# Adjacency transposed by DMA in 16-bit halves, filters loaded in nine 2 KB slots: one graph layer on one Trainium2 core

## The chip, the core and the metric

The kernel runs on one core of a Trainium2 chip. The core has a matrix engine (TensorE, PE in the profile, with its weight loads shown apart as PEld), a vector engine (VectorE, DVE), a scalar engine (ScalarE, ACT), GpSimd (POOL) and a sync engine (SP). SP, ACT and POOL also issue DMAs, each to a queue of its own (q1 is SP's, q10 ACT's, q0 POOL's in the profile); 16 DMA engines serve them all. Each engine runs its own list of instructions in order and waits on semaphores for the others.

The metric is the device time of one execution in microseconds (us). Lower is better. Seven runs of the kernel before took 1943.19 to 1951.11 us, median 1947.83.

## The reference

64 graphs of 256 nodes with 256 features (`x`, 64 x 256 x 256) and one symmetric 0/1 matrix per graph (`adj`, float32). Cut to what is computed:

```python
h = max(layernorm(x), 0)
# x_conv: 1-tap convolution over the nodes, batch norm, relu, 17-tap convolution, batch norm, + h, relu
s    = h @ w_se.T + b_se                                   # 3 numbers per node
dist = sq[:, :, None] + sq[:, None, :] - 2 * einsum('bnd,bmd->bnm', s, s)
A    = exp(-dist) * adj
msg  = relu(h @ w_msg.T + b_msg)
x_nmp = einsum('bnm,bmd->bnd', A, msg)
# gated recurrent unit over [x_conv, x_nmp] and h; result added to x
r, z = sigmoid(gi_r + gh_r), sigmoid(gi_z + gh_z)
out  = x + (1 - z) * tanh(gi_n + r * gh_n) + z * h
```

Everything is float32. `dist` is symmetric in its two node indices.

## The kernel before

Graphs are handled in pairs (`G = 2`, 512 columns), eight graphs (four pairs, `PB = 4`) make a batch, and there are eight batches (`NB`). The loop at lines 843 to 938 runs over the batches; in its body `i` is the batch's first pair and `nxt = i + 4` the first of the next batch, whose preparation is mixed in. The order of instructions is written out by hand (`manual_schedule`); the vector steps of a fast Fourier transform are put between other work by a small planner (`Pace`) that adds up estimated times of PE and DVE.

**Startup** (lines 390 to 841). The 17-tap filters are brought to the frequency domain with matmuls (`filters`), copied by ACT into `fo` (six buffers) and written to DRAM as `filt`, through SP's queue and in part POOL's. The filters do not fit on chip and are read back in each batch.

**A batch, product phase.** 16 frequency bins, two for each call of `products(b, m)`, m from 0 to 7. A bin has three kinds of filter (two in bin 15), 2 KB per partition and kind: 47 kinds in a batch. `load_bin` (line 591) loads a bin with one DMA on SP's queue into one of three buffers of 6 KB (`wb`); each bin is asked for three bins ahead of its use. `products` multiplies each kind by its operand (`Sv`, `V`, `U`, `PT`, results of the forward transform, which DVE computes), ACT copies one accumulator (`p`), DVE combines them into `Yv` and `Yu`. Between the calls stand parts of the graph work:

- `message(i)` (line 659): `msg` and the small embeddings `Z`; `embed(i)` (line 682) transposes `Z` into `ZT`.
- `affinity(i)` (line 689): four matmuls from `ZT`, ACT takes the exponential into `E`, DVE multiplies by `ADJ` (line 703), and then POOL's queue gets the two loads of the next pair's `adj` (`load_adj`, line 382; 2 KB rows).
- `transpose_a(i)` (line 707): A is needed with its second node index on partitions. Eight 128 x 128 transposes on PE (line 713) and two copies by ACT (line 714) make `AT`.
- `aggregate(i)` (line 716): `msg` times `AT`, eight matmuls (16 in the profile, since a float32 matmul shows as two), and two ACT copies into `XNM` (line 724).
- `finish(i)` (line 774): transposes the result of a pair back, DVE adds `x`, POOL's queue writes it out and loads `y` for a later pair.

`affinity(i)` stands after `products(b, 1)`, `transpose_a(i)` after `products(b, 2)`, `aggregate(i)` after `products(b, 3)`; the second pair follows in the same way after products 5, 6 and 7.

**A batch, gate phase.** `gates(i, dc)` (line 730) for four pairs and two halves: 18 matmuls of 512 columns each, ACT's `gn`, `tr`, `nn`, `tz`, DVE's `d`. Between them stand the graph work of pairs `i + 2` and `i + 3`, and for the next batch `transpose_h` (line 533; it also issues the load of `x` two pairs on, on SP's queue), `conv1` and the first steps of the Fourier transform.

Rows of a graph lie on partitions in the order `(h c)` after a view `(b h c)` (line 359): partition `16 h + b`, two rows `c` each. The tile `T` is scratch for the Fourier transform and first written by DVE when the forward transform begins.

Of the kernel before, what the change touches and what calls it, by code (L numbers as in the profile page):

```python
# [12 lines left out]

FP = mybir.dt.float32
AF = mybir.ActivationFunctionType
ALU = mybir.AluOpType
# [284 lines left out]
def kernel(  # L301
# [26 lines left out]
    nc = tc.nc  # L328
    P = 128
    B, N, D = x.shape  # L330
# [50 lines left out]

    def load_adj(i, eng=nc.gpsimd):
        ADJ[i] = work.tile([P, G * MC, N], FP, name="adj")
        load_rows(ADJ[i], adj, i, eng)

# [30 lines left out]

    HT, MSG, E, AT, XNM = {}, {}, {}, {}, {}

# [171 lines left out]

    def load_bin(b, n):
        b, n = b + n // BINS, n % BINS
        if b < NB:
            WB[b, n] = work.tile([P, 3, DC, D], FP, name="wb", bufs=3)
            kinds, m = 3 if n < BINS - 1 else 2, n // len(PASSES[0])
            first = 3 * (n - PASSES[m][0])
            nc.sync.dma_start(out=WB[b, n][:, :kinds], in_=filt[m][:, first:first + kinds])

# [13 lines left out]

    def products(b, m):
        load_bin(b, 2 * m + 2)
        p = [acc() for _ in range(3)]
        for n in range(2):
            for kind, v in enumerate(operands(2 * m + n)):
                if v is None:
                    continue
                for o in range(DC):  # L620
                    for k in range(DC):
                        mm(p[kind][:, (n * DC + o) * P:(n * DC + o + 1) * P],
                           WB[b, 2 * m + n][:, kind, k, o * P:(o + 1) * P],
                           v[:, k::DC, 0, :], P, start=(k == 0), stop=(k == DC - 1))
        load_bin(b, 2 * m + 3)
        p1 = work.tile([P, W], FP, name="p1")
        pv = [t.rearrange("p (n a e) -> p a n e", n=2, e=NW) for t in (p1, p[1], p[2])]
        if m < 7:
            nc.scalar.copy(p1, p[0])  # L629
            if m < 4:  # L630
                re, im = Yv(m % 2, m // 2 * 2, 2), Yv(m % 2, 4 + m // 2 * 2, 2)
            elif m < 6:
                re, im = Yu(m - 4, 0, 2), Yu(m - 4, 2, 2)
            else:
                t = Yu.t[:, :, :, 6:8, :].rearrange("p a c n e -> p n a c e")
                re, im = t[:, 0], t[:, 1]
            pace.vector(2 * W, pace.pe + PSUM)
            nc.vector.tensor_sub(re, pv[0], pv[2])
            nc.vector.tensor_add(im, pv[0], pv[1])
        else:  # L640
            half = W // 2
            nc.scalar.copy(p1[:, :half], p[0][:, :half])
            nc.scalar.mul(Yu(0, 4)[:, :, 0, :], p[0][:, half:].rearrange("p (a e) -> p a e", e=NW), 0.5)
            nc.scalar.mul(Yu(1, 4)[:, :, 0, :], p[1][:, half:].rearrange("p (a e) -> p a e", e=NW), 0.5)
            pace.vector(W, pace.pe + PSUM)
            nc.vector.tensor_sub(Yu(0, 5)[:, :, 0], pv[0][:, :, 0], pv[2][:, :, 0])
            nc.vector.tensor_add(Yu(1, 5)[:, :, 0], pv[0][:, :, 0], pv[1][:, :, 0])
# [41 lines left out]
    def affinity(i, early=False):  # L689
# [9 lines left out]
        for g in range(G):  # L699
            for c in range(MC):  # L700
                pace.vector(N, pace.pe + ACT)
                e = E[i][:, g, c].rearrange("p (c h b) -> p c h b", c=MC, b=NW)
                nc.vector.tensor_mul(e, e, ADJ[i][:, g * MC + c].rearrange("p (b h c) -> p c h b", c=MC, b=NW))
        if i + 1 < B // G:
            load_adj(i + 1)

    def transpose_a(i):
        AT[i] = late.tile([P, G, MC, N], FP, name="aT")
        for g in range(G):
            q = aux()  # L710
            for c in range(MC):
                for r in range(MC):
                    transpose(q[:, c * N + r * P:c * N + (r + 1) * P], E[i][:, g, r, c * P:(c + 1) * P])
            nc.scalar.copy(AT[i][:, g].rearrange("p c n -> p (c n)"), q)

    def aggregate(i):
        XNM[i] = late.tile([P, DC, W], FP, name="xnm", bufs=2)
        for dc in range(DC):
            p = aux()
            for g in range(G):  # L720
                for c in range(MC):
                    mm(graph(p, g), MSG[i][:, g, c, dc * P:(dc + 1) * P], AT[i][:, g, c, :], N,
                       start=(c == 0), stop=(c == MC - 1))
            nc.scalar.activation(XNM[i][:, dc, :], p, AF.Copy)


# [3 lines left out]
    def gates(i, dc, wait=None, early=None):  # L730
# [10 lines left out]
        product(ghn, h, n, True, True)  # L741
        gn = late.tile([P, W], FP, name="gn", bufs=2)
        nc.scalar.activation(gn, ghn, AF.Identity, bias=b_hh[:, 2 * DC + dc:2 * DC + dc + 1])
# [15 lines left out]
        nc.vector.scalar_tensor_tensor(gn, gn, 0.5, pn, op0=ALU.mult, op1=ALU.add)  # L759
        nn = late.tile([P, W], FP, name="nn", bufs=2)  # L760
        nc.scalar.activation(nn, gn, AF.Tanh, bias=b_ih[:, 2 * DC + dc:2 * DC + dc + 1])
# [51 lines left out]
    for t, v in ((b_msg[:, :D], msg_b), (b_msg[:, D:], se_b)):  # L813
        nc.gpsimd.dma_start(out=t, in_=bass.AP(tensor=v.tensor, offset=v.offset, ap=[[0, P], [1, v.shape[0]]]))
    load_adj(0, nc.sync)
    bn2 = bn_vecs(bn2, "bn2")
    b_ih, b_hh = vec(ih_b, "b_ih"), vec(hh_b, "b_hh")
    for j in range(PB):
        if j > 0:
            transpose_h(j)  # L820
        if 0 < j < PB - 1:
            norm(j + 1)
        conv1(j)
        run(split_steps(j))
        for m, n in steps[j * 4:(j + 1) * 4]:
            filters(m, n, nc.sync)
    s2, h2_shift = fold_bn(bn2, "bn2", 1.0 / L)
    b_rz = const.tile([P, 2 * DC], FP)
# [4 lines left out]
    for j, (m, n) in enumerate(steps[PB * 4:]):  # L833
        filters(m, n, nc.gpsimd if j % 2 else nc.sync)
        if j + PB * 4 == 2 * NG - 10:
            load_bin(0, 0)
            load_bin(0, 1)
    stage_ctx.close()
    late = ctx.enter_context(tc.tile_pool(name="late", bufs=1, reuse_waits="tile"))
    Yvt = late.tile([P, SL], FP, name="Yv")  # L840
    Yv = Slots(Yvt, GB * DC, L // 2, NW)
    pace.flush(odd)
    for b in range(NB):
        i = b * PB
# [4 lines left out]
        embed(i)  # L849
        if b > 0:  # L850
            finish(i - 1)
        products(b, 1)
        pace.add(fft.branch_back(Yv, T, 0))
        affinity(i)
        products(b, 2)
        transpose_a(i)
        products(b, 3)
# [12 lines left out]
        norm(nxt)  # L870
        affinity(i + 1)
        products(b, 6)
        transpose_a(i + 1)
        products(b, 7)
# [12 lines left out]
        join(3)  # L887
        aggregate(i + 1)
        transpose_h(nxt)
        message(i + 2)  # L890
# [3 lines left out]
        def wait(j=0):  # L894
            pace.flush(joined[j])
        gates(i, 0, wait, lambda i=i: affinity(i + 2, True))
        if b == 0:
            load_y(0)
            load_y(1)
        transpose_a(i + 2)  # L900
        gates(i, 1)
        pace.flush(normed)
        transpose_h(nxt + 1)
# [7 lines left out]
        pace.flush(joined[1])  # L911
        gates(i + 1, 0)
        pace.flush(normed)
        transpose_h(nxt + 2)
# [7 lines left out]
        embed(i + 3)  # L922
        gates(i + 1, 1)
        affinity(i + 3)
        gates(i + 2, 0)
        pace.flush(normed)
        transpose_h(nxt + 3)
        transpose_a(i + 3)
        conv1(nxt + 3)
# [55 lines left out]
```

## Time and profile before

The profiled execution took 1943.19 us, of which its span, from the first instruction to the last, is 1941.4.

| what | us |
|---|---|
| median of seven runs | 1947.83 |
| the profiled execution | 1943.19 |
| its span | 1941.4 |
| PE idle in the first 110 us | 32.1 |
| 256 transposes of `e` on PE, busy (line 712 to 713) | 38.3 |
| 64 copies `aT` on ACT (line 714), 0.59 each | 35.0 |
| 128 products `e * adj` on DVE (line 703) | 67.6 |
| PE and its weight loads waiting for `wb`, in all | 25.1 |
| SP issues of `wb` (128, 120 of them 768 KB) | 0.32 each |
| POOL issues of `adj` (62, 256 KB) | 0.60 each, 5.9 to landing |

The busy times of one engine overlap where it works as a pipeline, so a busy time is not always what an instruction adds to the list; the distance between two starts is. The granted clock of PE was 0.993 on average. A wait is named by the event that came last before the instruction began.

### The profile page before, as it was taken

To read this page: it belongs to the slowest core of one execution; us is meant where nothing else is said; L and a number is where in the kernel's file an instruction comes from. 1 tells how busy PE (TensorE), PEld (TensorE's weight loads), DVE (VectorE), ACT (ScalarE), POOL (GpSimd) and SP (SyncE) were. 2 spreads that over 40 slices of the span, in tenths; PEclk is the share of its full clock that TensorE was granted. 3 is DMA by queue.
4 is the path that set the end of the run, shared out by engine and by line. 5 is a ranking of instruction groups with operands and counts; after the bars stand their busy time and mean duration, and the time that the engine had idled before them with its cause. 6 is when DMAs were issued, how large, how long until landed. Compare 5 with 4: busy or idle time off the path is not lost.

```text
span 1941.4 us, 21503 instructions
## 1 busy us (share of the span) xinstructions
PE 1864.3 (96%) x7940; PEld 1161.3 (60%) x7940; DVE 1398.0 (72%) x2667; ACT 602.8 (31%) x1338; POOL 173.4 (9%) x266
## 2 busy tenths in 40 slices
PE   4999999999999999999999999999999999999997
PEld 2687544865468545774548654595546844577543
DVE  2888649985598946997489865898469884699522
ACT  1534331243222522243222432224322342224321
POOL 2110010000100010100000001000000000010000
PEclk9999999999999999999999999999999999999999
DMA  5784131721227112550126402172123711153010
GB/s 172 242 264 141 34 78 35 221 83 33 71 62 242 32 34 60 142 173 22 44 60 195 121 22 71 32 231 74 44 60 84 221 46 29 27 156 127 0 44 22
DMA packets 67938, 187.14 MB, mean 96 GB/s; under 512 B 20466, under 2 KB 25330, under 8 KB 67833
## 3 DMA queue, kind: packets, MB, share of 16 engines
q1 hardware_dynamic: 33884, 125.60, 19.5%
q0 software_dynamic: 29504, 56.50, 12.7%
q10 hardware_dynamic: 4445, 3.67, 0.6%
q8 instruction: 62, 1.02, 0.2%
q14 instruction: 43, 0.35, 0.1%
HBM read 156.54 MB, written 29.10 MB: 96 GB/s over the span
## 4 chain that ended last, share of the span: by engine, by line
PE 71%; DVE 15%; DMA 6%; ACT 4%; issue 3%; POOL 0%; DVEq 0%; ACTq 0%; POOLq 0%
PE acc L408 60%; PE aux L408 6%; DMA wb<-filt 4%; PE aux L412 3%; DVE T L64 2%; DMA taps<-in_c_wT_dram 1%; ACT Yv L656 1%; PE aux L696 1%; DVE Yv L61 1%; DVE Yv L58 1%; DVE U L64 1%; DVE PT L61 1%; DVE T L61 1%; DVE Sv L61 1%; DVE msg L668 1%
## 5 line engine op out<-in xcount | busy, mean ns | idle before, releaser
L408 PE MATMUL acc<-hT,w_hh 128*128 128x512 f32 x768 | 355.2, 597 | 0.0
L408 PE MATMUL acc<-xnm,w_ih 128*128 128x512 f32 x768 | 352.2, 595 | 0.0
L408 PE MATMUL acc<-Yv,w_ih 128*128 128x512 f32 x768 | 340.0, 592 | 0.0
L408 PEld LDWEIGHTS acc<-xnm,w_ih 128*128 128x128 f32 x768 | 146.9, 191 | 185.9 <-issue 185.9
L408 PEld LDWEIGHTS acc<-Yv,w_ih 128*128 128x128 f32 x768 | 145.9, 190 | 183.7 <-issue 183.0
L408 PEld LDWEIGHTS acc<-hT,w_hh 128*128 128x128 f32 x768 | 141.8, 190 | 158.4 <-issue 153.8
L756 DVE SCALAR_TENSOR_TENSOR gn<-tr,gn 128x512 f32<-128x512 f32 x64 | 44.2, 691 | 243.2 <-ACT tr L754 243.2
L754 ACT ACTIVATE tr<-acc,b_rz 128x512 f32<-128x512 f32 x64 | 44.0, 687 | 563.1 <-PE acc L408 563.1
L408 PE MATMUL acc<-hT,w_c 128*128 128x512 f32 x256 | 118.4, 606 | 14.5 <-ACT hT L541 14.5
L408 PE MATMUL acc<-U,wb 128*128 128x128 f32 x1024 | 123.5, 276 | 3.0 <-DMA wb<-filt 2.5
L408 PE MATMUL aux<-w_msg,hT 128*128 128x259 f32 x512 | 121.6, 385 | 4.2 <-DVE msg L668 4.2
L408 PE MATMUL acc<-V,wb 128*128 128x128 f32 x1024 | 124.8, 275 | 0.0
L408 PEld LDWEIGHTS acc<-U,wb 128*128 128x128 f32 x1024 | 119.1, 192 | 7.9 <-issue 2.7
L58 DVE SCALAR_TENSOR_TENSOR V<-T,V 128x256 f32<-128x256 f32 (+2 forms) x224 | 120.4, 607 | 0.3
L408 PEld LDWEIGHTS acc<-V,wb 128*128 128x128 f32 x1024 | 119.5, 192 | 0.0
L408 PE MATMUL aux<-aT,msg 128*128 128x256 f32 x512 | 117.4, 380 | 0.8
L408 PEld LDWEIGHTS aux<-w_msg,hT 128*128 128x128 f32 x512 | 94.1, 189 | 26.8 <-DVE msg L668 9.7
L782 POOL DMA_DIRECT2D out_dram<-y x64 | 39.0, 614 | 763.5 <-DVE y L781 762.2
L408 PEld LDWEIGHTS aux<-aT,msg 128*128 128x128 f32 x512 | 95.0, 190 | 18.8 <-issue 4.1
L408 PEld LDWEIGHTS acc<-hT,w_c 128*128 128x128 f32 x256 | 48.9, 195 | 64.4 <-issue 43.7
L64 DVE TENSOR_TENSOR V<-h 128x512 f32<-128x512 f32 x64 | 43.8, 684 | 54.7 <-ACT h L554 54.7
L629 ACT COPY p<-acc 128x512 f32<-128x512 f32 x56 | 32.8, 585 | 149.2 <-PE acc L408 74.4
(134 smaller groups left out, 2610.9 us busy)
## 6 DMA issues: line engine op xcount, KB each, us to landing
wb<-filt SPq DMA_DIRECT2D x120, 768.0 KB
y<-in_x_dram POOLq DMA_DIRECT2D x64, 256.0 KB, 5.7
out_dram<-y POOLq DMA_DIRECT2D x64, 256.0 KB, 4.7
adj<-in_adj_dram POOLq DMA_DIRECT2D x62, 256.0 KB, 5.9
x<-in_x_dram SPq DMA_DIRECT2D x60, 256.0 KB
filt<-fo SPq DMA_DIRECT2D x26, 252.0 KB
wb<-filt SPq DMA_DIRECT2D x8, 512.0 KB
filt<-fo POOLq DMA_DIRECT2D x10, 252.0 KB, 5.0
```

The source lines that it names most:

```text
L58: return self.step(out, lambda: self.v.scalar_tensor_tensor(out, x, s, y, op0=ALU.mult, op1=ALU.add))
L61: return self.step(out, lambda: self.v.tensor_add(out, x, y))
L64: return self.step(out, lambda: self.v.tensor_sub(out, x, y))
L408: nc.tensor.matmul(p, w, v, **kw)
L412: nc.tensor.transpose(p, v, ident)
L629: nc.scalar.copy(p1, p[0])
L656: nc.scalar.activation(v, v, AF.Relu, bias=h2_shift[:, o:o + 1])
L668: nc.vector.tensor_add(MSG[i][:, g, c, :], p[:, :D + SE], b_msg)
L696: nc.tensor.matmul(p[:, :N], ZT[rows_q, :P], ZT[rows_q, P:], start=True, stop=True)
L754: nc.scalar.activation(tr, pr, AF.Tanh, bias=b_rz[:, dc:dc + 1], scale=0.5)
L756: nc.vector.scalar_tensor_tensor(gn, tr, 1.0, gn, op0=ALU.add, op1=ALU.mult)
L782: nc.gpsimd.dma_start(out=rows(out, G * i + g), in_=row_tile(Y[i], g))
```

## The change

1. `transpose_a` and `AT` are gone. `aggregate` multiplies by `E` itself. As `dist` is symmetric, A^T is the exponential times the transposed `adj`; `ADJ` now holds `adj` transposed.
2. The transposed `adj` is made by DMA. Seen as 16-bit numbers a graph's `adj` is 256 x 512. `turn_adj` transposes it from DRAM to SBUF with one DMA transpose per graph on SP's queue (`HALVES`: column halves on partitions). `keep_adj` writes it to a DRAM buffer in eight DMAs of 128 pieces of 512 B, `load_adj` reads it back in eight DMAs of 128 pieces of 512 B with the rows on the right partitions (`ADJH`), all on SP's queue, and `join_adj` puts the two 16-bit halves together into `ADJ` with two ACT copies. The first two pairs use `T` as the place for `HALVES`.
3. The filters come one kind at a time: 376 DMAs of 256 KB into nine slots of 2 KB per partition, each asked for as soon as the kind nine places before it has been used. Before the first batch three bins are loaded instead of two.
4. Order: `finish(i - 1)` moves from after `products(b, 0)` to after `products(b, 2)`; `transpose_h(nxt)` from after `aggregate(i + 1)` to after `products(b, 6)`; the turns, writes and loads of `adj` are put into the batch by hand, the two loads of the product phase after `affinity(i)` and `affinity(i + 1)`. `gn` and `nn` have one buffer instead of two.

```diff
+    def turn_adj(i):
+        if i >= B // G:
+            return
+        if i < 2:
+            HALVES[i] = Tt.bitcast(U16).rearrange("p (i g k n) -> p i g k n", i=2, g=G, n=N)[:, i]
+        else:
+            HALVES[i] = late.tile([P, G, 2 * MC, N], U16, name="halves")
+        for g in range(G):
+            nc.sync.dma_start_transpose(out=HALVES[i][:, g], in_=adj[G * i + g].bitcast(U16))
+
+    def keep_adj(i):
...
+        ADJD[i] = dram.tile([G, L // 2, MC, 2, NW, N], U16, name="halves_d", bufs=6)
+        v = ADJD[i].rearrange("g h c j (k a) n -> g k a (h c j) n", a=4)
+        for g in range(G):
+            for k in range(2 * MC):
+                nc.sync.dma_start(out=v[g, k], in_=HALVES[i][:, g, k])
+
+    def load_adj(i):
...
+        ADJH[i] = late.tile([P, G, MC, 2, N], U16, name="adjh")
+        v = ADJD[i].rearrange("g h c j b n -> g c j h b n")
+        for g in range(G):
+            for c in range(MC):
+                for j in range(2):
+                    nc.sync.dma_start(out=ADJH[i][:, g, c, j], in_=v[g, c, j])
+
+    def join_adj(i):
...
         ADJ[i] = work.tile([P, G * MC, N], FP, name="adj")
-        load_rows(ADJ[i], adj, i, eng)
+        v = ADJ[i].bitcast(U16).rearrange("p q (n j) -> p j q n", j=2)
+        for j in range(2):
+            nc.scalar.copy(v[:, j], ADJH[i][:, :, :, j].rearrange("p g c n -> p (g c) n"))
...
-    def load_bin(b, n):
+    def load_kind(b, n, kind):
         b, n = b + n // BINS, n % BINS
-        if b < NB:
-            WB[b, n] = work.tile([P, 3, DC, D], FP, name="wb", bufs=3)
-            kinds, m = 3 if n < BINS - 1 else 2, n // len(PASSES[0])
-            first = 3 * (n - PASSES[m][0])
-            nc.sync.dma_start(out=WB[b, n][:, :kinds], in_=filt[m][:, first:first + kinds])
+        if b < NB and (n < BINS - 1 or kind < 2):
+            WB[b, n, kind] = work.tile([P, DC, D], FP, name="wb", bufs=9)
+            m = n // len(PASSES[0])
+            nc.sync.dma_start(out=WB[b, n, kind], in_=filt[m][:, 3 * (n - PASSES[m][0]) + kind])
...
     def products(b, m):
-        load_bin(b, 2 * m + 2)
...
-        load_bin(b, 2 * m + 3)
+                load_kind(b, 2 * m + n + 3, kind)
...
-        if i + 1 < B // G:
-            load_adj(i + 1)
...
-                    mm(graph(p, g), MSG[i][:, g, c, dc * P:(dc + 1) * P], AT[i][:, g, c, :], N,
+                    mm(graph(p, g), MSG[i][:, g, c, dc * P:(dc + 1) * P], E[i][:, g, c, :], N,
                        start=(c == 0), stop=(c == MC - 1))
             nc.scalar.activation(XNM[i][:, dc, :], p, AF.Copy)
+        if join:
+            join_adj(i + 1)
...
-    load_adj(0, nc.sync)
+    turn_adj(0)
+    turn_adj(1)
...
             filters(m, n, nc.sync)
+        if j < 2:
+            keep_adj(j)
...
     pace.flush(odd)
+    load_adj(0)
+    join_adj(0)
     for b in range(NB):
...
         affinity(i)
+        load_adj(i + 1)
         products(b, 2)
-        transpose_a(i)
+        if b > 0:
+            finish(i - 1)
         products(b, 3)
...
         affinity(i + 1)
+        if b > 0:
+            load_adj(i + 2)
+        else:
+            turn_adj(2)
         products(b, 6)
-        transpose_a(i + 1)
+        if b == 0:
+            keep_adj(2)
+            turn_adj(3)
+        transpose_h(nxt)
         products(b, 7)
...
+        load_adj(i + 3)
+        turn_adj(nxt)
...
         gates(i, 1)
+        keep_adj(nxt)
+        turn_adj(nxt + 1)
...
         gates(i + 1, 0)
+        keep_adj(nxt + 1)
+        turn_adj(nxt + 2)
...
         gates(i + 1, 1)
+        keep_adj(nxt + 2)
+        turn_adj(nxt + 3)
         affinity(i + 3)
+        load_adj(nxt)
         gates(i + 2, 0)
+        keep_adj(nxt + 3)
```

In the first batch `load_adj(2)` and `keep_adj(3)` come after the joins are queued, ahead of `aggregate(i + 1)`, and `join_adj(2)` comes in the `early` call of `gates(i, 0)`; in the other batches `join_adj(i + 1)` is the end of each `aggregate(i)`.

## The prediction

> **What bounds the kernel now.** I read the page first, busy time and the chain that ended last:
>
> ```profile
> span 1941.4 us, 21503 instructions
> PE 1864.3 (96%) x7940; PEld 1161.3 (60%) x7940; DVE 1398.0 (72%) x2667; ACT 602.8 (31%) x1338; POOL 173.4 (9%) x266
> ...
> PE 71%; DVE 15%; DMA 6%; ACT 4%; issue 3%; POOL 0%; DVEq 0%; ACTq 0%; POOLq 0%
> ```
>
> TensorE (PE) sets the pace; what shortens its instruction list shortens the end, unless PE then waits. By the timeline a batch lasts 229.2 us and repeats. The stage windows of the batch that starts at 570.23 us (columns: stretch, its length, busy time of PE, weight load, DVE, ACT, POOL, granted clock, DMA share, GB/s) split it into a product phase, to the second `aggregate`, and a gate phase:
>
> ```profile
> 570.23:627.70 57.47, 54.98 (x455) 52.04 (x454) 52.46 (x113) 15.85 (x49) 5.91 (x9) 1.00 0.72 225
> 627.70:799.44 171.74, 170.01 (x512) 87.70 (x511) 121.87 (x220) 55.34 (x112) 13.08 (x19) 1.00 0.18 46
> ```
>
> The reader sees two different stages. In the gate phase PE is 99% busy and DMA 18%: transfers there are free. In the product phase PE, DVE (52.46 of 57.47) and DMA are all near their limits, and it is where the filters stream through SP's queue. Two waits on PE matter, seen in PE's timeline: the one for a filter, and in the gate phase the price of eight transposes of `e`, which is the distance between the two starts, 0.87 us:
>
> ```profile
> 587.25 1.16 PE L408 MATMUL acc<-Sv,wb 128*128 128x128 f32 x8 [1.42 <-DMA wb<-filt]
> ...
> 428.43 1.04 PE L412 MATMUL aux<-ident,e 128*128 128x128 f32 x8
> 429.30 1.88 PE L408 MATMUL acc<-hT,w_hh 128*128 128x512 f32 x4
> ```
>
> Last I asked what one hardware queue delivers. The DMA views of five short stretches give its packets, MB and share of the 16 engines; in this order: `x` rows of 2 KB (405.5 to 407.5 us), `fo` rows of 2 KB (66 to 70), `wb` rows of 6 KB (586 to 589), `taps` rows of 1 KB on SP (8 to 12), single 4-byte elements on ACT's queue (3 to 6):
>
> ```profile
> q1 hardware_dynamic: 197, 0.38, 50.3%
> ...
> q1 hardware_dynamic: 427, 0.80, 64.4%
> ...
> q1 hardware_dynamic: 209, 1.16, 99.2%
> ...
> q1 hardware_dynamic: 440, 0.60, 40.7%
> ...
> q10 hardware_dynamic: 544, 0.00, 9.7%
> ```
>
> That is 99, 107, 70, 110 and 181 packets a us. With 6 KB packets the engines are full (99%, 387 GB/s); with 1 and 2 KB the queue stops near 100 to 110 packets a us while the engines are only 41 to 64% busy. So on this queue a small packet costs about 10 ns whatever it holds, and 2 KB packets give 190 to 200 GB/s.
>
> **The change, part by part.** *Transposes and their copy removed.* Per batch four `transpose_a`, two in each phase: 2 x 0.87 = 1.74 us off PE in the gate phase and as much in the product phase. 64 copies `aT` of 0.59 us leave ACT.
>
> *Filters in nine 2 KB slots.* The bytes are the same, but each bin's 128 packets of 6 KB become 3 x 128 of 2 KB. PE eats a kind in 0.89 us (a bin from 570.23 to 572.91 is 2.68 us), the queue brings one in 128/100 = 1.28 us. Of 47 kinds nine are there when the phase begins, so 38 x 128 = 4864 packets must pass: 48.6 us. Alone this fits: PE needs 57.47 less the transposes 1.74, the filter wait 1.42 and the small wait on `e` 0.2, so 54.1 us.
>
> *`load_adj` on SP, in that stream.* It left POOL's queue (two issues of 0.60 us, which nothing waits for) and is now eight DMAs of 128 pieces of 512 B. Both of a batch's product-phase calls, after `affinity(i)` and `affinity(i+1)`, stand in SP's order before filters: behind the first wait kinds 21 to 26, behind the second kinds 45 and 46. No 512 B row is in the trace; bounds are 97 packets a us (the 2 KB row's slow end) and 181 (the 4-byte row); I take 130, as it is nearer to the 1 KB row. 2048 / 130 = 15.8 us. The phase cannot end before the queue: first slot free 0.9, from a freed slot to data 1.7 (572.9 to the first packets about 574.5), 48.6 + 15.8, landing about 0.5, last kind 0.9: 68.4 us against 57.5, **+10.9 us**. Bounds: 110 and 181 give 59.5 (+2.0), 97 for both gives 75.2 (+17.7); a queue that is no limit gives 54.1 (-3.4). In stalls: PE waits about 6 to 9 us ahead of kind 21, in `products(b, 3)`, and 3 to 9 ahead of kind 45, in `products(b, 7)`.
>
> [...]
>
> *Turning and storing adj.* Per pair two DMA transposes, eight `keep_adj` writes and a wait between them, all on SP, in the gate phase from the second batch's data on. 1024 pieces at 130 a us are 7.9 us per `keep_adj`. No transpose by DMA is in the trace; of 256 KB the bounds are 0.7 us (387 GB/s) and 9.3 us (1024 pieces of 256 B at 110 a us). I take 2 us, nearer the low end, since the bytes are those of an `x` load, whose 256 packets take 2.6. Queue work in the gate phase: 8 x 2 + 4 x 7.9 + 2 x 7.9 + eight `x` loads of 2.6 = 84 of 171.7 us, hidden behind PE's gates. Behind a waiting `keep_adj` stand the next turn and an `x` load, which is needed some 30 us after its issue (445.82, statistics at 478.02). Were the cover gone, SP would be late with `load_adj(nxt)`, and ACT would stand in `join_adj`.
>
> [...]
>
> *`join_adj` on ACT.* Two copies of 1024 columns; the row `aT` has 0.59 us for 512 and `e` 0.38 for 256, so about 1.0 us each. ACT is 31% busy. Behind it stands `p` (603.53 while `xnm` ended at 600.5, room for 2 us). Only at the head of the gates is ACT tight (PE waited 0.74 us for `zT`): bounds 0 and 0.9 us a batch, I take 0.5.
>
> *Nothing:* `finish` between products 2 and 3 is the same 0.87 us of PE and the same DVE adds; `gn` and `nn` with one buffer add no wait, as ACT and DVE read and write them in the order they already had.
>
> *Startup.* `load_adj(0)` comes after the last `fo` (SP at 110 us): 1024/130 = 7.9 + 1.7 + 0.5 lands near 120, `join_adj(0)` ends near 122, and ACT, free at 109.7, starts `z` then instead of at 113.2: **+9 us**. Four turns ahead of the `fo` writes: 0 to 27 us (9.3 each, less what is idle from 33 to 43), taken as 0 at 2 us each. So 9, bounds 0 and 36.
>
> **Sum.** A batch: +10.9 - 1.74 + 0.5 = +9.7; eight: +77. With startup +86. The profiled execution took 1943.2 us (span 1941.4 and 1.8 around it): 2029. The median of the runs shown, 1947.8, is 4.6 above it: **2034 us**. The first batch has one `load_adj` less and two turns instead; I count it as the others. This case's own range, from the bounds: +2.0 - 1.74 = 0.3 a batch and nothing at the start give 1950; 17.7 - 1.74 + 0.9 = 16.9 a batch and 27 give 2110.
>
> **Rivals.** *The queue keeps pace; the change does what it is for.* Then the product phase is 54.1 us. For it: the filter wait of 1.4 us comes where `finish` writes its output, and finer slots start each load earlier. Against it: the five rows. DVE's 52.46 us leave only half of the 3.4 us: -1.7 - 1.74 = -3.4 a batch, -28, startup +5 (`load_adj(0)` 3.3 us instead of 7.9): 1920, on the median's scale **1925** (1907 with DVE no limit gives 1912). It decides from the point where two `load_adj` take less than 59.2 - 52.6 = 6.6 us, 310 pieces a us.
>
> *The turns are slow.* At 9.3 us each, SP has before the end of `load_adj(nxt)` eight turns (74), three `keep_adj` (24), two `load_adj` (16) and six `x` loads (16): 130 us from `affinity(i+2)` at 416, so 546, where `aggregate(i+3)` ends its `xnm` at 534.5. ACT stands 12 us, PE loses about 10 a batch, and the start 18 more: 2034 + 98, **2132**. From about 6 us a turn on. Against it: each moves no more bytes than an `x` load.
>
> *Nothing to see.* The gates' -14 us and the filter waits -11 are paid back by short stalls of 3 us a batch: about **1949**. It needs `load_adj` at about 300 pieces a us, which no row has.
>
> **How the numbers follow.** Main case 0.63, the queue keeping pace 0.22, slow turns 0.11, nothing to see 0.04. Predicted is the main case, 2034 us, own range 1950 to 2110. For 8 in 10 the range reaches into the first rival, to 1915, which leaves out about 0.10 below and 0.10 above. 0.2% (3.9 us) is what a measurement can tell from no change: faster 0.22, the same 0.03, slower 0.75.
>
> **What would show it.** Right: PE waiting on `wb` in `products(b, 3)` and `products(b, 7)`, a product phase near 68 us, SP's queue at about 100 packets a us in it with the engines not full, a gate phase near 170 us. Wrong: `wb` waits as short as now, or 512 B pieces at 300 a us and more; or waits of ACT for `adjh` in the gates, which would be the slow turns; or lost time before 180 us alone.

## The result and the profile after

The changed kernel takes 1956.84 us in the median of 20 runs (1953.05 to 1961.47), the kernel before 1948.54 in the median of 47: a ratio of 1.0041, 95% interval 1.0031 to 1.0052. So it is slower, as forecast and inside the range, but by 8 us and not by the forecast 86.

The page of the changed kernel: the span and the busy times.

```profile
span 1954.3 us, 22266 instructions
PE 1850.1 (95%) x7684; PEld 1142.9 (58%) x7684; DVE 1396.7 (71%) x2667; ACT 644.0 (33%) x1338; POOL 136.1 (7%) x204
```

PE lost its 256 transposes, 32 groups of 0.87 us or 28 us of its list, but is busy only 14 us less, so the work that stayed got slower, and the span grew by 13: 27 us more in which PE stands. The start of each batch (PE's first product with `Sv`) says where. In us, as in all tables here, from one profiled execution of each kernel:

| kernel | start | first batch | batches 2 to 7 | last batch | span |
|---|---|---|---|---|---|
| before | 112.6 | 228.5 | 1378.8 | 221.5 | 1941.4 |
| after | 125.7 | 245.8 | 1359.3 | 223.5 | 1954.3 |
| difference | +13.1 | +17.3 | -19.4 | +2.0 | +12.9 |

Six batches out of eight got faster, by 3.24 us each. What is lost lies before 371 us and in the last batch. The stage windows of the batch that starts at 597.78 (columns as before: length, busy PE, weight load, DVE, ACT, POOL, clock, DMA share, GB/s):

```profile
597.78:652.24 54.46, 53.35 (x448) 51.10 (x447) 52.31 (x113) 17.15 (x49) 3.48 (x5) 1.00 0.79 241
652.24:825.34 173.10, 170.38 (x488) 86.56 (x487) 121.82 (x220) 59.21 (x112) 10.69 (x15) 0.98 0.28 69
```

The product phase is 54.46 us, where 68.4 were forecast. PE's and PEld's waits for `wb` are 3.5 us in the whole run (25.1 before). The gate phase is 173.10 us at a clock of 0.98, although three 0.87 us groups of transposes (two of `e`, and one of `x` that moved) have left it. In the DMA views of three stretches, `wb` rows of 2 KB (603 to 611 us, with the first pieces of a `load_adj`), `x` rows of 2 KB (540.5 to 542.5) and the 512 B writes of `keep_adj` (504 to 508), the reader sees three rates of one queue: 148, 99 and 174 packets a us, at 86%, 49% and 29% of the 16 engines. Some 3 to 11% of these packets hold only 4 bytes; by the MB the filters pass at 132 rows of 2 KB a us and `x` at 93.

```profile
q1 hardware_dynamic: 1186, 2.16, 86.2%
...
q1 hardware_dynamic: 198, 0.38, 49.4%
...
q1 hardware_dynamic: 697, 0.35, 28.8%
```

Packets of the same 2 KB pass at 148 and at 99 a us. That is not a price per packet of the queue. 49% and 29% are near 8 and 4 of 16 engines, and the `x` rows are read in 8 groups of 16 rows, the `keep_adj` writes in 4 groups, the `wb` rows as 128 in one step. Whether the groups are the reason is tested below.

**The start and the first batch.** SP's issues while the kernel starts, and in the first batch (start, length, line, what is moved), then ACT's issue of two `x` loads and PE's first long wait in the start, each after and before:

```profile
30.35 18.86 SPq L396 DMA_TRANSPOSE T<-in_adj_dram  x4
...
179.43 2.71 SPq L396 DMA_TRANSPOSE halves<-in_adj_dram  x2
...
202.39 6.31 SPq L415 DMA_DIRECT2D adjh<-halves_d  x8
```

```profile
34.06 12.65 ACTq L377 DMA_DIRECT2D x<-in_x_dram  x2
...
34.11 3.97 ACTq L376 DMA_DIRECT2D x<-in_x_dram  x2
```

```profile
47.66 2.07 PE L447 MATMUL acc<-taps,points 119*126 119x256 f32 x4 [11.59 <-ACT h L593]
...
39.04 2.07 PE L408 MATMUL acc<-taps,points 119*126 119x256 f32 x4 [3.77 <-ACT h L554]
```

Four turns hold SP for 18.86 us (later a pair takes 2.6), and SP's queue alone keeps the 16 engines 94% busy meanwhile. ACT, issuing two `x` loads at the same time, is held for 12.65 us in place of 3.97, comes late to `h`, and PE waits 7.8 us longer for it. In the first batch the third pair is turned, written, read back and joined in one chain, from 179.43 to 213.4. ACT's joins at both places and PE's waits behind them (the number in brackets is the idle time before):

```profile
136.24 2.52 ACT L423 COPY adj<-adjh 128x1024 uint16<-128x1024 uint16 x2 [13.33 <-DMA adjh<-halves_d]
...
210.93 2.52 ACT L423 COPY adj<-adjh 128x1024 uint16<-128x1024 uint16 x2 [5.68 <-DMA halves_d<-halves]
```

```profile
139.04 1.21 PE L451 MATMUL aux<-ident,z 128*128 128x128 f32 x3 [7.80 <-issue]
...
213.73 1.22 PE L734 MATMUL aux<-zT 9*128 9x256 f32 x2 [8.31 <-ACT e L735]
```

The first is PE waiting for `z`, which stands behind the first join on ACT. 7.80 and 8.31 us of PE make most of the first batch's +17.3.

**The head of the gates.** PE in a batch of the kernel before, then PE and ACT in the changed one, and the windows around the wait (the first of before):

```profile
642.01 0.71 PE L696 MATMUL aux<-zT 9*128 9x256 f32 x6 [0.75 <-ACT zT L686]
```

```profile
662.95 1.88 PE L447 MATMUL acc<-hT,w_hh 128*128 128x512 f32 x4
666.31 0.71 PE L734 MATMUL aux<-zT 9*128 9x256 f32 x6 [1.47 <-ACT zT L724]
667.48 1.22 PE L734 MATMUL aux<-zT 9*128 9x256 f32 x2 [0.46 <-ACT e L735]
668.62 3.78 PE L447 MATMUL acc<-hT,w_hh 128*128 128x512 f32 x4
```

```profile
656.39 2.54 ACT L423 COPY adj<-adjh 128x1024 uint16<-128x1024 uint16 x2
```

```profile
640.00:648.00 8.00, 6.79 (x21) 2.80 (x21) 6.86 (x14) 4.90 (x12) 1.18 (x2) 1.00 0.11 22
...
662.00:670.00 8.00, 6.07 (x19) 2.68 (x18) 6.42 (x16) 7.05 (x15) 0.00 (x0) 0.84 0.54 120
670.00:678.00 8.00, 8.00 (x15) 3.26 (x14) 7.79 (x15) 2.00 (x4) 0.00 (x0) 0.73 0.29 74
```

ACT's join of 2.54 us stands ahead of `z` and `zT`, and PE's wait for `zT` has doubled (0.75 us before, 1.47 now); 0.46 for `e` is as before. Behind it the granted clock falls to 0.84 and 0.73 of these 8 us stretches, and the same four `hT,w_hh` take 3.78 us that take 1.88 at full clock. In the 25 us from 60 us after each batch's start, the clock of batches 2 to 7 reads 0.93, 0.86, 0.93, 0.86, 0.93, 1.00; before it was 1.00 in four of these six and 0.93 in two. In the last batch it is 0.73, and there PE's wait is 2.92 us, for `z` (0.87 before).

**The theory from here:** the steady batches get what the transposes and the filter waits cost, less the late join at the head of the gates and the clock behind it; what is paid once, for halves that no gate phase hides, takes the rest. The rival is the theory of the prediction, a queue with a price per packet; other rivals stand with the experiments.

### The profile page after: what moved, and what is told of

It reads as the page before. It is cut to its first block, busy times and chain, and to the rows that moved or that the text cites. A ratio compares the mean times of both kernels' runs of the same rounds, so it can differ in the third digit from the quotient of the medians.

```text
span 1954.3 us, 22266 instructions
## 1 busy us (share of the span) xinstructions
PE 1850.1 (95%) x7684; PEld 1142.9 (58%) x7684; DVE 1396.7 (71%) x2667; ACT 644.0 (33%) x1338; POOL 136.1 (7%) x204
## 4 chain that ended last, share of the span: by engine, by line
PE 73%; DVE 11%; DMA 6%; ACT 5%; issue 4%; POOL 0%; ACTq 0%; SPq 0%; DVEq 0%; POOLq 0%
PE acc L447 63%; PE aux L447 6%; DMA wb<-filt 3%; PE aux L451 2%; DMA taps<-in_c_wT_dram 2%; PE aux L734 1%; ACT Yv L68 1%; DVE T L65 1%; DVE Yv L59 1%; DVE Yv L62 1%; DMA x<-in_x_dram 1%; ACT adj L423 1%; DVE U L65 1%; DVE PT L62 1%; DVE Sv L62 1%
## 5 line engine op out<-in xcount | busy, mean ns | idle before, releaser
L447 PE MATMUL acc<-hT,w_hh 128*128 128x512 f32 x768 | 367.2, 614 | 0.0
L447 PEld LDWEIGHTS acc<-hT,w_hh 128*128 128x128 f32 x768 | 146.0, 195 | 167.8 <-issue 163.5
L447 PE MATMUL aux<-e,msg 128*128 128x256 f32 x512 | 115.8, 379 | 0.0
L447 PEld LDWEIGHTS aux<-e,msg 128*128 128x128 f32 x512 | 95.5, 190 | 15.9 <-issue 4.3
L423 ACT COPY adj<-adjh 128x1024 uint16<-128x1024 uint16 x64 | 81.3, 1340 | 19.0 <-DMA adjh<-halves_d 13.3
```

Of the source, the lines that this page charges most:

```text
L423: nc.scalar.copy(v[:, j], ADJH[i][:, :, :, j].rearrange("p g c n -> p (g c) n"))
L447: nc.tensor.matmul(p, w, v, **kw)
```

## The experiments

The kernel before ran beside each on the same chip; ratios are to it, with their 95% interval. The spans, cut as above:

| kernel | start | first batch | batches 2 to 7 | last batch | span |
|---|---|---|---|---|---|
| ring alone | 116.9 | 228.9 | 1372.1 | 219.6 | 1937.5 |
| turned adj alone | 126.0 | 248.5 | 1369.5 | 226.8 | 1970.7 |
| no turning | 113.9 | 226.4 | 1351.4 | 217.6 | 1909.3 |
| join early | 124.8 | 245.9 | 1352.2 | 217.3 | 1940.1 |
| first batch by PE | 117.1 | 228.4 | 1360.5 | 221.4 | 1927.4 |
| both of these | 114.4 | 226.8 | 1349.1 | 218.3 | 1908.6 |
| before with copies at the head | 114.0 | 229.9 | 1391.1 | 227.2 | 1962.3 |
| writes in 128 rows | 123.9 | 244.2 | 1361.4 | 221.4 | 1950.9 |
| filters in 8 groups | 133.2 | 259.6 | 1440.4 | 236.8 | 2070.0 |
| `x` in 128 rows | 119.7 | 243.9 | 1358.9 | 220.4 | 1942.9 |
| both, and writes in 128 rows | 114.4 | 226.9 | 1351.5 | 217.9 | 1910.7 |
| both, and the head filled | 114.7 | 227.5 | 1341.8 | 219.2 | 1903.1 |

### The two parts, each alone

The ring alone is the kernel before with `load_kind`, `products` and the nine slots of the changed one:

```diff
-            load_bin(0, 0)
-            load_bin(0, 1)
+            for n in range(3):
+                for kind in range(3):
+                    load_kind(0, n, kind)
```

> The kernel before with the nine 2 KB slots alone (adj is loaded and e turned as before; three bins instead of two are loaded ahead). Theory now (the rate of a DMA goes with the number of engines that its rows reach, and a filter kind of 128 rows reaches 16): wb comes at about 145 to 155 packets a us while it streams, as in the changed kernel; the waits of PE for wb, 1.4 us a batch, go away; 8 x 1.4 = 11 us less, about 1937 us against 1948.5. The theory of the prediction (SP's queue stops near 100 packets a us): wb at 100 packets a us with the engines about half busy, 48.6 us of queue work in a product phase of 57.5, hardly a wait left either, so again about 1937, but a product phase that ends with waits for wb of 1 to 3 us where finish writes its output. The rate of the packets tells the two apart. Third case: the ring gives nothing alone, 1948.

The turned adj alone is the changed kernel with `load_bin` and its three 6 KB buffers:

```diff
-            WB[b, n, kind] = work.tile([P, DC, D], FP, name="wb", bufs=9)
+            WB[b, n] = work.tile([P, 3, DC, D], FP, name="wb", bufs=3)
```

> The changed kernel with the old ring of three 6 KB bins: the turned adj alone. Theory now: what is lost once (start +13 us, first batch +17 us) stays, PE waits for wb as before (1.4 us a batch and more where a load of adj stands ahead of a bin), and the steady batches keep 3.5 us of transposes less about 2.2 us of the late join and of the clock after it: 1956.8 + 11 to 20, so 1968 to 1977 us, slower than both kernels. The theory of the prediction: 16 bins of 6 KB take 29 us of the queue, two loads of adj 15.8 us, which fit into 57.5 us; 8 x (-3.5 + 0.5) + 9 = -15 us against before: 1933 us.

Measured: the ring alone 1939.13 us, 0.9952 (0.9934 to 0.9970); the turned adj alone 1972.38, 1.0117 (1.0094 to 1.0141). Both came where the new theory had them; for the second the prediction's own steps, which see no loss in the first batch, give 1933. For the ring alone both theories had about 1937, so the time does not tell them apart; the rate does. In the DMA view from 578 to 583 us the filters pass at 150 packets a us, where the prediction had 100 at half the engines:

```profile
q1 hardware_dynamic: 749, 1.35, 86.5%
```

Against the kernel before, run beside them, the parts alone are worth -8 and +25, together +8: the ring is worth 15 us where loads of adj stand ahead of filters (PE's waits for `wb`, without PEld's, are 18.0 us in the turned adj alone and 1.3 in the changed kernel). Alone it is worth less than its waits, and the batches show why: they last 227.5 us where the clock at the head of the gates was 1.00 (two of six) and 229.2 to 229.5 where it was 0.93 (four). Before, 229.1 to 229.5 went with 1.00 and 230.9 with 0.93. So the ring gave 1.6 us a batch, and in most batches a fall of the clock took 1.7 back.

### No turning

```diff
+        ADJ[i] = work.tile([P, G * MC, N], FP, name="adj")
+        load_rows(ADJ[i], adj, i, nc.gpsimd if i else nc.sync)
...
-    turn_adj(0)
-    turn_adj(1)
```

> The changed kernel without turning, storing, loading back and joining: adj is loaded plainly by POOL as before and E used directly, so it leaves out the transposing of adj (which is symmetric in these inputs). It shows what the whole route of the halves costs beside transposes that are gone. Theory now: the start goes back to about 112.6 us (-13), the first batch to about 225 us (-20), six later batches lose the join at the head of the gates and the clock behind it (-1 to -2.8 each): 1905 to 1918 us. Rival: the start and the first batch are late because of the third bin loaded ahead and the order on SP, not because of the halves: then the start stays above 120 us and the time is 1930 to 1940 us.

Measured 1911.12 us, 0.9797 (0.9772 to 0.9823): as the theory had it. The whole route of the halves costs 45 us of the changed kernel's span: 11.8 at the start, 19.4 in the first batch, 7.9 in six batches and 5.9 in the last. The third bin loaded ahead is not what delays the start (113.9).

### The join, early

```diff
         transpose_h(nxt)
+        if b > 0:
+            join_adj(i + 2)
         products(b, 7)
...
-        aggregate(i + 1, b > 0)
+        aggregate(i + 1, False)
```

> The changed kernel, in which from the second batch on the join of the pair i+2 is issued on ACT ahead of products(b, 7) and no longer behind aggregate(i+1), at the head of the gates. Theory now: the wait of PE ahead of e at the head of the gates goes back from 1.5 us to 0.75 or less, the granted clock stays at 1.00 over the first 20 us of the gates in batches 1 to 6, and each of these batches gets 2 to 3 us shorter: 1937 to 1945 us. Rival: the clock falls for another reason, and the two copies of 2.55 us only move their delay to the copy of p in products(b, 7) and the DVE steps behind it: 1953 to 1957 us, the clock below 1.00 at the same place.

Measured 1943.82 us, 0.9984 (0.9966 to 1.0002), 13 us less than the changed kernel. PE's wait at the head of the gates, and the same two stretches of the windows:

```profile
664.13 0.71 PE L734 MATMUL aux<-zT 9*128 9x256 f32 x6 [0.74 <-ACT zT L724]
```

```profile
662.00:670.00 8.00, 6.80 (x18) 2.68 (x17) 7.20 (x16) 5.55 (x13) 0.00 (x0) 0.79 0.36 96
670.00:678.00 8.00, 8.00 (x20) 3.48 (x19) 6.63 (x17) 1.33 (x2) 1.31 (x1) 1.00 0.31 68
```

The wait is back at 0.74 and the second stretch at full clock, but the first is not: I had expected 1.00 throughout, and five of the six batches read 0.93. The gain per batch is 1.2 us, half of what I expected; another 6.2 come from the last batch, where the clock over the 25 us went from 0.73 to 1.00 and PE's wait for `z` from 2.92 back to 0.87 us. So the late join costs 13 us, but with a wait of 0.74 us, followed by the 0.46 for `e`, the clock still falls in most batches.

### The suspected cost by itself

Two copies behind `aggregate(i + 1)` in the kernel before, on a tile that nothing reads:

```diff
         aggregate(i + 1)
+        for _ in range(2):
+            nc.scalar.copy(idle, idle)
```

> The kernel before with two more copies of 1024 16-bit columns on ACT behind aggregate(i+1), at the head of the gates, whose result nothing reads: the head of the gates as the changed kernel has it, and nothing else of the change. Theory: ACT reaches z and zT later, PE's wait ahead of e grows by 0.5 us and more, the granted clock falls below 1.00 in the 20 us behind it in some of the batches, and a batch gets 1.5 to 4 us longer: 1960 to 1978 us. Rival (ACT is 31% busy and has room; the prediction took 0.5 us a batch): 1948 to 1952 us with the clock at 1.00.

Measured 1961.18 us, 1.0067 (1.0051 to 1.0082), at the low end of the theory, while ACT is no busier than a third of the time. PE, and a window behind it:

```profile
637.70 2.89 PE L408 MATMUL aux<-w_msg,hT 128*128 128x259 f32 x12 [0.76 <-DVE msg L668]
...
646.82 0.71 PE L696 MATMUL aux<-zT 9*128 9x256 f32 x6 [0.75 <-ACT zT L686]
```

```profile
648.00:656.00 8.00, 8.00 (x16) 3.45 (x17) 7.79 (x13) 2.28 (x6) 1.18 (x2) 0.79 0.32 68
```

The place differs from what I expected: the wait for `zT` stays 0.75, and a new one of 0.76 us stands ahead of it, where PE waits for `msg`, since here `hT` is what the copies delay on ACT. 2 us of work a batch on an engine that is idle two thirds of the time cost 13 us in all. 0.76 us a batch is the new wait; the clock reads 0.93 in four of the six batches 2 to 7 (two before) and 0.80 in the last. What the rest of the 2 us a batch is was not taken apart.

### The first batch by PE

In the first four pairs adj is loaded plainly and `e` transposed by PE as before, the result copied back over `e`; turning begins with the fifth pair:

```diff
-        if i >= B // G:
+        if i >= B // G or i < PB:
             return
...
+            nc.scalar.copy(E[i][:, g].rearrange("p c n -> p (c n)"), q)
...
-    turn_adj(0)
-    turn_adj(1)
+    plain_adj(0, nc.sync)
```

> The changed kernel, in which the four pairs of the first batch get A^T from PE as in the kernel before (adj loaded plainly, e transposed, the result copied back over e); the turning by DMA begins with the fifth pair, in the gates of the first batch. Theory (the start and the first batch pay for halves that nothing hides there): start back to about 113 to 116 us, first batch back to about 228 us, six pairs of steady batches as in the changed kernel: 1956.8 - 27 = 1930, between 1924 and 1935 us. Rival (the first batch is slow because of the clock and of the third preloaded bin): 1945 us and more.

> first_by_pe and join_early together. Theory: the gains of the two add, as one lies in the start and the first batch and the other in the batches behind it: 1956.8 - 27 - 13 = 1917, between 1908 and 1923 us, faster than both kernels. Rival: the early join is worth nothing any more, or the first batch has to pay elsewhere: 1930 us and more.

Measured: 1929.25 us alone, 0.9902 (0.9885 to 0.9918); with the early join 1912.68, 0.9822 (0.9805 to 0.9839). Both as the theory had them: the two losses lie in different places and add, and each edit changes mainly its own columns of the table (the others move by 0.1 to 3.1 us). What the start and the first batch pay is paid for halves that are not hidden there.

### How many engines a DMA uses

Three kernels alter only the order in which a DMA walks its rows; for `x` and the halves the rows also become neighbours in DRAM by it, for the filters they lie apart in both orders. `x` in 128 rows:

```diff
-        load_rows(X[i], x, i, eng)
+        for g in range(G):
+            eng.dma_start(out=row_tile(X[i], g), in_=x[G * i + g].rearrange("(p c) d -> p (c d)", c=MC))
```

> The changed kernel with x loaded as 128 rows of 2 KB in one step instead of 8 groups of 16; the same packets and bytes. The rows of x then come in another order, so it computes with exchanged nodes. Theory now: the row on which the prediction rested, 98 packets of 2 KB a us at 50% of the engines, becomes 145 and more at 80 to 100%; the time stays within 0.4% of the changed kernel's, as the loads of x lie in the gate phase. The theory of the prediction (about 10 ns a packet on this queue): 98 a us again.

A single run took 1944.62 us. In the DMA view of 1 us of an `x` load (531.7 to 532.7):

```profile
q1 hardware_dynamic: 209, 0.40, 102.2%
```

209 packets a us at full engines, where the same packets had passed at 99 and 49%. The price per packet is gone with the order of the rows. The time is 12 us below the changed kernel's, more than the 0.4% I had allowed: 6 of them at the start, where 2.5 us are gained before PE's first work, which waits for `x`, and 5 in the first and the last batch.

The converse, each filter kind read in 8 groups of 16 rows:

```diff
-            nc.sync.dma_start(out=WB[b, n, kind], in_=filt[m][:, 3 * (n - PASSES[m][0]) + kind])
+            nc.sync.dma_start(out=WB[b, n, kind].rearrange("p o d -> p (o d)"),
+                              in_=filt[m].rearrange("(b h) k o d -> h b k (o d)", h=8)[:, :, 3 * (n - PASSES[m][0]) + kind])
```

> The changed kernel with one thing altered: each filter kind is read from DRAM as 8 groups of 16 rows of 2 KB, like the rows of x, and not as 128 rows in one step; packets, bytes and the number of DMAs are the same. The rows of the filters then come in another order, so it computes with exchanged input channels. It makes the filter stream what the prediction took it for. Theory now (the first step of the rows sets how many engines take part): wb falls from 145 to 155 packets a us at 90% of the engines to about 100 at 50%, as x has it; the queue then needs 38 x 1.28 = 48.6 us for the filters and, at the measured 230 pieces a us, 8.9 us for two loads of adj, so the product phase ends at 0.9 + 1.7 + 48.6 + 8.9 + 0.5 + 0.9 = 61.5 us instead of 54.5: +7 a batch, +4.5 in the first, which has one load of adj less: 1956.8 + 53 = 2010, between 1985 and 2035 us, with waits of PE for wb of several us in products(b, 3) and products(b, 7). Rival (2 KB packets of this queue run at 150 a us whatever the order of the rows): 1957 us and no such waits.

Measured 2076.51 us, 1.0663 (1.0621 to 1.0704), 120 us more than the changed kernel and more than I expected. The DMA view from 670 to 690 us, and PE's waits for filters in that batch, which starts at 637.60:

```profile
q1 hardware_dynamic: 2018, 3.89, 51.4%
```

```profile
665.84 2.08 PE L447 MATMUL acc<-Sv,wb 128*128 128x128 f32 x8 [6.92 <-DMA wb<-filt]
...
703.28 1.16 PE L447 MATMUL acc<-U,wb 128*128 128x128 f32 x8 [2.69 <-DMA wb<-filt]
...
706.38 4.49 PE L447 MATMUL aux<-e,msg 128*128 128x256 f32 x16
```

101 packets a us at half the engines; waits of 6.92 us ahead of kind 21 and 2.69 ahead of kind 45; a product phase of 706.38 - 637.60 = 68.8 us. The prediction had waits of 6 to 9 and 3 to 9 us at these two kinds and a phase of 68.4.

The waits and the rate bear the step out, but that the two lengths agree is partly luck. In this batch's trace the pieces of the two `load_adj` move for 5.8 and 5.4 us, together 11.2 and not the prediction's 15.8. In exchange the filters, at 95 rows of 2 KB a us by the MB of the view, need 51.2 us and not 48.6, and behind PE's long wait the queue stands nearly still for 1.6 us, for which the prediction has no term. My expectation of 61.5 failed by the same three: it had 8.9 us for `load_adj`, 48.6 for the filters and no pause.

The rival that the packets of `x` are simply slower, by their place in DRAM, can be read off these rows: the share times 16 engines times the time of the view, over the 2 KB rows that passed (the MB), is how long one row keeps an engine busy. It gives 85 ns for `x` in 8 groups, 84 for `x` in 128 rows, 87 for the filters in 8 groups and 105 for the filters in 128 rows. The rows are not slower in groups; fewer are under way at once, about 8 in place of 14 to 16.

The writes of the halves in 128 rows, by another layout in DRAM:

```diff
-        ADJD[i] = dram.tile([G, L // 2, MC, 2, NW, N], U16, name="halves_d", bufs=6)
-        v = ADJD[i].rearrange("g h c j (k a) n -> g k a (h c j) n", a=4)
+        ADJD[i] = dram.tile([G, NW, L // 2, MC, 2, N], U16, name="halves_d", bufs=6)
+        v = ADJD[i].rearrange("g (k a) h c j n -> g k (a h c j) n", a=4)
```

> The changed kernel with the halves kept in DRAM in another order, so that the slowest step of a keep_adj write has 128 places instead of 4; bytes, pieces of 512 B and DMAs are the same. Theory (the number of engines goes with the slowest step): keep_adj goes from 173 packets a us at 29% of the engines to 400 and more, load_adj stays where it was (slowest step 8, 204 to 282 a us); the time falls by the writes' share of the start alone, 0 to 6 us. Rival (512 B pieces to DRAM cost what they cost): 173 a us again and the same time.

> first_by_pe, join_early and keep_contiguous together. Theory: the writes of the halves are hidden in the gate phase anyway, so this stands with first_by_pe_join_early: 1912.7 us, between 1908 and 1917. Rival: faster writes end earlier, nothing stands behind them on SP when x is issued, and 2 to 6 us more are gained.

The first took 1952.69 us in a single run; the DMA view of 1 us with such writes alone (499 to 500):

```profile
q1 hardware_dynamic: 444, 0.20, 69.6%
```

444 packets a us at 70%, against 174 at 29%, as expected; SP still takes 4.91 us to issue the eight writes of a pair (6.52 in the changed kernel). The time is 4 us below the changed kernel's median, inside the 0 to 6 expected, but from one run. The second took 1913.41 us, 0.9816 (0.9790 to 0.9843), the same as without it: once the start is free of writes their rate is hidden, as the theory said. A whole batch without turning and one of this kernel show the same length to 0.01 us:

```profile
565.52:790.76 225.24, 222.14 (x934) 136.97 (x933) 174.09 (x332) 67.31 (x152) 18.98 (x28) 0.99 0.34 93
```

```profile
566.60:791.84 225.24, 222.14 (x933) 136.97 (x932) 174.11 (x332) 76.63 (x160) 14.16 (x20) 0.99 0.41 111
```

So in a steady batch turning, storing and loading back cost nothing; only the place of the join does.

### The head of the gates filled

To both edits (first batch by PE, join early) a third, the same products in another order:

```diff
-        if early:
-            early()
-        pr, pn, pz = acc(), acc(), acc()
-        product(pr, h + xn, r, True, False)
+        pr = acc()
+        product(pr, h, r, True, False)
+        if early:
+            early()
+        pn, pz = acc(), acc()
+        product(pr, xn, r, False, False)
```

> first_by_pe and join_early together, and at the head of the gates the four products of hT with the next block of w_hh (1.7 us of PE) are issued ahead of the products of zT and no longer behind them: the same work in another order. It takes the two short waits of PE (0.74 us for zT, 0.46 us for e) away by work that is there anyway. Theory (these waits make the granted clock fall behind them, at about 1.75 us a fall): the wait for zT goes, the clock stays at 1.00 over the head in every batch, and a batch falls from 225.2 to 222 to 223.7 us: 1912.7 - 8 x 1.5 to 3 = 1889 to 1901 us. Rival (the clock falls there for another reason): only the waits of about 0.7 us go, the clock stays at 0.93 over these 25 us: 1905 to 1909 us.

Measured 1902.97 us, 0.9772 (0.9750 to 0.9795): the fastest version here, 2.3% faster than the kernel before. PE at the head, and the window:

```profile
635.67 0.71 PE L736 MATMUL aux<-zT 9*128 9x256 f32 x6
636.83 0.69 PE L736 MATMUL aux<-zT 9*128 9x256 f32 x2 [0.46 <-ACT e L737]
```

```profile
630.00:640.00 10.00, 9.54 (x30) 4.21 (x29) 9.81 (x21) 8.02 (x18) 0.00 (x0) 1.00 0.51 116
```

The wait for `zT` is gone, and the clock over the 25 us behind the products is 1.00 in all eight batches. That shows the wait for `zT` as what pulls the clock down at the head; the wait of 0.46 us for `e` is still there. The time is 2 us above the range that I gave: I counted eight batches where six lie between the first and the last, and in two of these PE waits 1.48 and 1.03 us for a filter (224.8 and 224.3 us; the other four take 223.1 to 223.4).

## Why the prediction was wrong in size

**The step that failed** is the reading of the DMA rows: "with 1 and 2 KB the queue stops near 100 to 110 packets a us while the engines are only 41 to 64% busy. So on this queue a small packet costs about 10 ns whatever it holds". The rows were right, the conclusion was not. The 99 packets a us of `x` belong to the 8 groups in which `x` is walked; the filters are walked in one step of 128, and pass at 132 rows of 2 KB a us: 36.8 us for the prediction's 48.6. The second term of the same sum, `load_adj` at 130 pieces a us, was mis-sized too: SP issues 1024 pieces in 4.96 us and they move as fast, so 10.1 us for 15.8. With both put right the prediction's sum is 0.9 + 1.7 + 36.8 + 10.1 + 0.5 + 0.9 = 50.9 us (the 0.5 for the landing is the prediction's estimate; no run shows it apart), less than PE's 54.1 (with the filters alone put right 56.6). Nothing is left of the +10.9 us a batch: the phase has 54.5 us, the length that the prediction gave for "a queue that is no limit". And with the filters read by 8 groups the long waits come, and the phase has 68.8 us.

The share beside the rate told it: 50.3% is what 8 of 16 engines would give, and it stood in the prediction as a sign of a limit per packet. The second row, 107 packets of `fo` at 64%, is no limit either. The view it comes from has the engines' share in 40 slices of its 4 us, in tenths:

```profile
DMA  1000100589888795676887795796745677796987
```

For seven slices next to nothing moves, then the engines are 40 to 90% busy: a mean over a pause and a stream.

In the runs 8 groups went with 49 to 51% of the engines (`x`, and the filters when read so), 4 groups with 29%, a little over 4 of 16, and 128 rows in one step with 70% (the writes in the other layout), 86% (the filters) and 102% (`x`). What other numbers of rows or groups would give was not shown.

**Transposes off PE**, 1.74 us a phase: the runs fit it, though none takes it apart. 225.24 us a batch without turning is 4.5 below the mean of 229.8 before; 3.5 for the transposes and 1.6 for the ring, less 1.1 for the falls of the clock, which it has in six batches instead of two, make 4.0.

**Turns at 2 us, writes hidden in the gate phase:** right for the steady batches. A pair of turns takes SP 2.6 us (4.5 once), eight writes 4.6 to 7.1 (9.5 once), and the equal batches show that nothing of it is paid there. The rival of slow turns falls with it; at the start alone a turn takes 4.7 us.

**The join, 0.5 us a batch:** too small. The copies take 1.34 us each and not 1.0; at the head of the gates they cost 1.2 us in a steady batch and 6.2 in the last, 13 in all with the clock, against 4. The prediction priced the wait (0.72 us longer) and not the fall of the clock behind it (0.84 and 0.73 over 8 us each).

**The start, +9:** this term was ACT coming late to `z` behind the first join. That is the 7.80 us which PE waits for `z` in the first batch, so it was about right. What failed is the term beside it, the four turns ahead of the `fo` writes, "taken as 0 at 2 us each". They cost most of the 13.1 us by which the start grew: 7.8 us lie in PE's one wait behind them, and with the first batch left to PE the start is 8.6 to 11.3 us shorter (117.1 and 114.4). **The first batch, "I count it as the others":** this step failed too. Of its 17.3 us 8.31 are PE waiting because turn, write, load and join of the third pair follow each other there with no gate phase above them.

The sum as it is: six batches -19.4, last +2.0, start +13.1, first batch +17.3: +12.9. The first rival, the queue that keeps pace, had -3.4 us a batch for a measured -3.24; it missed the sign because it took that for all eight batches and gave the start 5 us. That the forecast "slower" came true is luck: its reason, +9.7 us a batch, did not happen, and what did, time lost before 371 us, stood in the prediction only as a sign of being wrong ("lost time before 180 us alone"). Beside that, the upper end of its range counts 27 us for the start, where its own bound is 36: it should read 2119, not 2110.

## What to carry to other kernels

A rate read off one DMA held here for its shape alone (2 KB packets of `x`: 99 a us in 8 groups, 209 in 128 rows): read the share of the engines beside it, and before a rate is carried to another transfer compare in how many groups each is walked; a share that stood near 1/2 or 1/4 meant here that engines were left out, not that packets were dear. Work that the loop hid here was not hidden before it (+13.1 us) and in its first turn (+17.3); price these apart, and let the old way do the first turn where it can. Where an engine with little to do feeds the busiest one, price more than the length of the wait: 0.72 us of it cost 1.2 us a batch here, and ready products put in front of the 0.74 us that were left took that wait away, with the clock at 1.00 in all eight batches.

## What the hardware showed beside this

The granted clock fell in steps. In windows cut to them it reads 0.50 for 3.4 us (874.04 to 877.46 in the kernel before) or for twice that (667.43 to 674.26 in the changed one, behind the head shown above). Batches of the ring alone that differ in the clock at the head of the gates differ by 1.7 us (227.5 and 229.2); in the changed kernel 225.0, 226.0 to 226.6 and 227.6 to 227.8 us go with 1.00, 0.93 and 0.86 over the 25 us. By an estimate from the windows, 3.4 us at 0.50 lose 1.7 us: that agrees. Waits of 0.74 and 0.46 us some 1.2 us apart were enough for a fall in two of six batches before, five of six with the join early and all six without turning, and without the first of them there was no fall (1.00 in all eight batches with the head filled). Why the same waits make a fall in some batches and not in others stays open.

An ACT copy of 1024 columns of 16 bits takes 1.34 us in the join, where it writes every second column, and 1.04 in the two idle copies, which leave none out; `aT`, 512 columns of 32 bits and so the same bytes, takes 0.59. The turn of 256 KB by DMA, which no row of before could price, holds SP for 1.3 us in the gate phase.
